# Four GNN layers over 64 graphs on one core: layer 3's transposes written to DRAM in one piece, the last graph's end in halves, new ranks for the planner, and the second graph's exponentials transposed through DRAM

## The chip, the cores and the metric

The kernel runs on one core of a Trainium2 chip. The time is the device time of one execution in microseconds (us). Before the change it is 2665.98 us, the median of three runs (2665.81 to 2669.04).

## The reference

64 graphs, each with 256 nodes, 256 features and a 256 x 256 adjacency matrix, go through four layers. Each layer computes x = layernorm(x + layer(x, adj)), all in float32.

```python
# layer 0: 4 heads, sigmoid attention scaled by degree
att = sigmoid(q @ k.T * hd ** -0.5); adj_h = adj[:, None] * att
dis = deg ** -0.5                       # deg = adj_h.sum(-1)
y = layernorm((dis[:, None] * adj_h * dis[None, :]) @ leaky(x @ W + b)) * g + b
# layer 1: 8 heads, softmax masked by adj > 0
y = softmax(where(adj > 0, q @ k.T / sqrt(hd), NEG)) @ v @ Wo + bo
# layer 2: y = silu(rmsnorm((eps * x + adj @ x) @ W1 + b1) * w) @ W2 + b2
# layer 3: one head
e = leaky(s1[:, None] + s2[None, :], 0.2)
y = gelu(layernorm(softmax(where(adj > 0, e, NEG)) @ (x @ W)) * gamma + beta)
```

## The kernel before

A graph's 256 nodes are two blocks of 128 partitions. `graph` (L340) writes down the operations of one graph with `op(engine, cost, fn, writes, reads, ...)`; nothing is emitted yet. `Plan.order` (L184) then plays all 64 graphs through a list scheduler: for each engine it keeps a clock, it takes the ready operation with the smallest key (start time plus `LEAD`, then due time plus `RANK`), and `emit` (L845) issues the operations in the order of their planned starts. So the order on every engine, SP's queue of DMAs included, is fixed by the costs in the `op` calls, by the tables `RANK` and `LEAD` (one number for each kind of operation), by `AHEAD`, `STAY`, `TURN_STAY` and by the buffers in `SLOTS`. Each engine runs its own list in that order and waits on semaphores; a late operation holds up all that stand behind it.

In the middle of the run the order is periodic: all four layers are on the way at once, each for another graph. TensorE (PE) runs float32 matmuls of 128 x 256 in two passes. Some of its operations use only a part of the array's rows or columns: L550 (scores of layer 0, 64 rows), L631 (scores of layer 1, 32 rows, two halves of 8 matmuls), L568 (degrees, 32 columns), L590 (layer 0's product, 64 columns), L667 (layer 1's product, 32 columns), L733 (mean square of layer 2, 32 columns). L365 is a transpose by PE. All others (L421, L432, L702, L714, L755, L770) use the full array. The planner adds `CHANGE` when PE goes from one of these modes to another, and `join` (L142) can tie an L733 to the L631 of another graph.

Which line makes what: L421 q and k of layers 0 and 1 (and v, output and attention products by `token_major`, L432); L702 adj @ x; L714 and L755 the two matmuls of layer 2; L770 x @ W of layer 3, with the two columns for s1 and s2; `normed` (L460) is the layer norm: L445 the statistics on VectorE (DVE), L453, the power -0.5 on GpSimd (POOL) at L455, L464, and the scaling on ScalarE (ACT) at L468; `plus` (L482) adds the residual.

A transpose is made in one of two ways. By PE: `transposed` (four 128 x 128 transposes into PSUM) and an ACT `copy`. Or through DRAM: `far_transposed` (L373) transposes 32 x 32 blocks on DVE (L377), writes them to a DRAM tile `far` and reads them back in another order. For layer 3 (`in_order=True`) these are four writes (L383) and four reads (L387); for layer 0's y one write (L391) and four reads (L393). Layer 1's exponentials take the same way for a pair of heads: DVE L652, one write L654, four reads L656. `NEAR = 1, 2, 3` says which graphs go by PE instead: the first one in layer 0, the first two in layer 1 (L640 to L648), the last three in layer 3 (L761, L784).

The end of a graph is L785 to L792: the product of layer 3, `stats`, `affine`, gelu, the sum with x, `normed` and the output's write, each over all 256 nodes at once. For the last three graphs (`ENDS`) ACT does a part of DVE's work (L468, L493).

Of the kernel before, what the change touches and what calls it, by code (L numbers as in the profile page):

```python
# [9 lines left out]
AF = mybir.ActivationFunctionType  # L10
OP = mybir.AluOpType

P = 128
# [16 lines left out]
AHEAD = 12.7  # L30
STAY, TURN_STAY = 197, 988
NEAR = 1, 2, 3
# [7 lines left out]
SLOTS = {"s": 42, "d": 10, "b": 3, "c": 72, "p": 8, "h": 8, "t": 5, "w": 3, "f": 8}  # L40
DRAM = "hf"

RANK = [
    3.44, -1.34, 0, 0.79, 3.63, 0, 7.06, 0, 0, 2.3, -1.09, 0.34, 2.1, 0.78, 0.47, 0, -8.07, 0, -2.5, 0, 15.95,
    3.93, 0.83, -0.82, -4.23, -2.95, 1.61, -7.35, 4.27, 6.06, 1.96, 5.09, -16.2, 5.57, 0.49, -0.6, 0, 0.29, 0.2,
    0, 8.07, 0, 0.26, 0, 0, -8.02, -0.52, 0.34, -5.71, 0, 1.06, -2.37, 0.99, -8.94, 0, 0, -4.56, -2.34, -6.61,
    0.36, 0.84, -1.13, 0.53, 4.6, -1.2, -1.71, 0, 0, 0, -0.62, 4.15, -3.45, -2.5, -0.12, 6.63, 0.18, 0, 0.38,
    -0.79, -2.84, 0, -12.65, 1.3, 0, -1.96, 1.34, -1.62, 20.11, -1.52, 0, -0.8, -2.32, -1.64, 0, -1.22, -15.66,
    0, -6.95, -2.98, 0, 0.05, -1.56, -0.82, -0.77, -6, -2.56, -2.91, -11.65, -5.25, -1.35, -5.62, 0.33, 0, 0.59,
    -0.44, -28.89, -6.83, 0, 0.4, 0, 0.46, 0.76, 0, 0, 12.94, -5.14, 4.78, 3.27, 0.41, -2.4, -1.34, 0, -0.87,  # L50
    -1.92, 0, -2.52, 0, -10.08, -2.01, 3.32, 0.57, -18.67, -3.41, 0, 4.56, 5.08, 3.05, -3.62, 0, 3.39, -0.48,
    -0.64, -0.1, -3.66, 19.76, -6.53, 16.91, 0, -3.84, -1.2, 0.37, -12.68, 0, -6.52, 5.03, 11.31, 6.22, 1.25,
    -5.4, 5.28, 9.76, 2.05, -0.81, -6.1, 0.74, -0.33, -6.78, -1.35, 0.27, 2.67, -2.73, 0.77, -0.98, -12.61, 0,
    1.81, 1.44, 1.4, -0.43, -5.6, 1.17, 0, -3.52, -0.14, -0.86, -0.05, -0.51, 0, 25.51, 0, 0, 0, -2.88, 0, 0, 0,
    -0.4, -0.07, 0, 0, 2.29, 0, 0, -2.22, -0.14, 1.6, 0.52, -0.32, -2.95, 0, 0, 0, -0.56, 0, -0.75, 8.73, 0, 0,
    0, 0.27, 9.58, -7, 0.78, 1.68, 0, -0.23, -10.25, -9.94, 0, 2.37, 3.11, -1.12, 0.31, -0.32, 0, -2.88, -2.04,
    0, -2.34, -0.49, -1.73, -1.73, -3.1, -1.77, 1.2, -3.97, 0.04, -0.58, -3.77, -19.26, 1.61, 0, 2.15, 0, 1.75,
    -9.45, 0, -11.3, -4.22, -40.55, -11.19, -1.7, 0, -1.02, 20.28, 2.54, 0, 0, -11.95, -3.71, 4.81, 4.78, 0, 1.6,
    0, 0, 0, -4.09, 0, -20.33, 0.55, 0.76, 0, 0, -5.26, 0.23, 2.23, 0.95, 0.44, -0.83, -0.57, -4.63, -0.68,
    -0.52, 11.56, 0.73, 0, 0, 5.95, 1.53, -1.94, 0, 1.27, 0.18, 0, -0.41, -3.03, -5.78, -1.03,  # L60
# [3 lines left out]
    0, 0, 0, 4, 0, 21, 963, 0, 0, 0, 63, 0, 36, -156, 0, 241, -51, 5, -54, -409, 0, 480, 0, -31, 0, 0, -1244, 5,  # L64
    0, 581, -13, 104, -75, 53, 0, 0, 0, 0, 0, 0, 0, 0, 0, 0, 0, 100, 0, 0, 0, 0, -88, -216, 0, -127, 0, 0, 0, 0,
    0, 0, 0, 0, 0, 0, 0, 0, 0, 0, 0, 0, 0, 73, 0, -648, -13, 0, 0, 0, 0, 0, 243, 0, 0, 0, 0, 0, 0, 52, 0, 0, 0,
    0, 0, 0, 0, 0, 0, -1022, -191, 0, 0, 0, -79, 0, 13, -157, 0, 0, 0, 0, 0, 0, 0, 0, 0, 0, 0, 0, 0, 0, 0, 0, 0,
    0, -14, -96, -46, -142, 175, -7, -49, -988, -8, 0, 0, 0, 0, -3, 56, -31, 223, 0, 72, -40, -885, 811, -10, 0,
    0, 0, 0, -181, 559, -5, 0, 0, 323, 144, 0, 239, -109, 0, 0, -40, 0, -97, -886, 230, 144, -105, 0, 2, -92, 38,
    -275, 0, 0, 0, 0, 0, -262, 0, 0, 0, -468, -319, 0, 0, 0, 0, -390, 256, 267, 0, 0, 0, 0, 0, 42, 0, 0, 0, 0, 0,  # L70
    -325, 0, 0, 0, 0, 0, -236, 0, -117, -279, 0, 0, -1, 0, 0, 0, 0, 0, 0, 0, 0, -14, 0, 0, 0, 0, 0, 0, 0, 0, 0,
    0, 0, 0, 0, 0, 0, -261, -256, 0, 0, 0, 0, 0, 0, 0, 0, -139, 0, 0, 37, 0, 0, 0, 0, 0, -156, 0, 0, 0, 0, 0, 0,
    0, 0, 0, -25, 0, 262, -10, 105, 0, 0, 0, 0, 0, -34, -107, -53, -189, -141, -364, 0, 0, -161, -46, -115, 0,
    -12, 0, -883, 0, 0, 0, 0, 0, 0, -109, -14, 0, 187, 0, -13, 721, 0, 0, -68, -68, 0, -58, 0, -31, 417, 0, 227,
]

# [40 lines left out]
class Plan:  # L117
# [66 lines left out]
    def order(self):  # L184
# [17 lines left out]
        while ready:  # L202
            best = None
            for op in ready:
# [10 lines left out]
                for kind, n in need.items():  # L215
                    free = self.free[kind]
                    if len(free) < n:
                        break
                    start = max(start, sorted(free)[n - 1][0])
                else:  # L220
                    key = start + LEAD[op.rank], op.due + RANK[op.rank], op.graph, op.index
                    if best is None or key < best[0]:
                        best = key, start, op
# [116 lines left out]
def graph(plan, nc, c, t, out, b):  # L340
# [14 lines left out]
    def load(name, src):  # L355
        v = Value("s", name, 2)
        op("SP", 470, lambda: nc.sync.dma_start(two(v), t[src][b].rearrange("(n p) d -> p n d", p=P)), [v], after=5000, size=256)
        return v
# [14 lines left out]
    def far_transposed(src, name, in_order=True):  # L373
# [509 lines left out]
```

## Time and profile before

| what | value |
|---|---|
| median of three runs | 2665.98 us |
| the profiled execution's own time | 2665.97 us |
| its span, first to last instruction | 2664.2 us |
| PE busy (matmuls) | 2629.6 us, 17248 records |
| DVE busy | 2463.8 us |
| ACT busy | 2246.5 us |
| POOL busy | 640.5 us |
| DMA packets | 764628, 502.48 MB |
| weight load of 128 x 128 (L714), mean | 190 ns |
| DVE 32 x 32 transposes of 128 x 512 (L377), mean | 671 to 713 ns |

The page's first part gives busy times; its second cuts the span into 40 slices and shows the busy share of each engine in tenths; its fourth part follows the chain that ended last. The windows view gives busy times by stretch, the timeline shows instructions in order of time with their starts, and the waits view lists who waited for whom. A matmul record has a modelled end and overlaps the next, so the work on PE is read here from the distances between starts.

### The profile page before, as it was taken

The page shows a single profiled execution, that of the slowest core. Times are in us where ns is not written, and L with a number is a line of the kernel's source. Part 1 is how long each engine was busy: PE and PEld are TensorE (multiplying, and loading weights), DVE is VectorE, ACT ScalarE, POOL GpSimd, SP SyncE. Part 2 cuts the span into 40 slices and gives each one's busy share as a digit, 9 for nine tenths or more (in the row PEclk, how much of TensorE's full clock was granted, in tenths as well). Part 3 has the DMA queues.
Part 4 walks back from the last instruction along what each step waited for, and adds up shares of the span by engine and source line. Part 5 has one row for each costly group of instructions (what it writes and reads, how often), then busy time and mean ns, then how long its engine had stood idle before and what let it go on. Part 6 is the DMA issues. An engine that isn't in the chain of part 4 may idle for free.

```text
span 2664.2 us, 54927 instructions
## 1 busy us (share of the span) xinstructions
PE 2629.6 (99%) x17248; PEld 2122.6 (80%) x17248; DVE 2463.8 (92%) x6905; ACT 2246.5 (84%) x5343; POOL 640.5 (24%) x1029
## 2 busy tenths in 40 slices
PE   8999999999999999999999999999999999999997
PEld 6777888888887888888888878878888887877786
DVE  6799999999999999999999999999999999989976
ACT  4888888888888888988888888889889888888886
POOL 1122222222222222222222222222222222222222
PEclk9999999999999999999999999999999999999998
DMA  4577777776777777777767777777677776676761
GB/s 142 153 210 199 196 206 188 200 202 182 210 195 187 197 200 192 200 189 200 200 187 206 196 186 202 196 188 200 193 195 203 188 199 183 178 198 186 212 162 38
DMA packets 764628, 502.48 MB, mean 189 GB/s; under 512 B 383792, under 2 KB 724144, under 8 KB 764336
## 3 DMA queue, kind: packets, MB, share of 16 engines
q1 hardware_dynamic: 764336, 498.97, 69.7%
q8 instruction: 137, 2.24, 0.4%
q14 instruction: 155, 1.27, 0.2%
HBM read 301.35 MB, written 197.39 MB: 187 GB/s over the span
## 4 chain that ended last, share of the span: by engine, by line
PE 89%; DVE 5%; DMA 2%; SPq 1%; issue 1%; ACT 1%; POOL 1%; POOLq 0%; DVEq 0%; ACTq 0%
PE ps L432 16%; PE ps L755 15%; PE ps L421 15%; PE ps L714 15%; PE ps L631 5%; PE ps L702 4%; PE ps L550 4%; PE ps L590 4%; PE av L667 4%; PE ps L770 4%; PE ps L365 1%; PE ps L568 1%; DVE mv L445 1%; DVE e L513 1%; DMA eT<-far 1%
## 5 line engine op out<-in xcount | busy, mean ns | idle before, releaser
L518 ACT ACTIVATE e<-e,low 128x256 f32<-128x256 f32 x1152 | 576.4, 503 | 156.9 <-DVE low L513 150.9
L455 POOL TENSOR_TENSOR mv<-mv,mhalf 128x2 f32<-128x2 f32 x384 | 313.7, 822 | 965.7 <-DVE mv L453 759.8
L714 PE MATMUL ps<-aggT,w 128*128 128x256 f32 x2048 | 463.8, 379 | 0.0
L755 PE MATMUL ps<-w,hT 128*128 128x256 f32 x2048 | 456.4, 380 | 0.0
L755 PEld LDWEIGHTS ps<-w,hT 128*128 128x128 f32 x2048 | 387.8, 190 | 56.1 <-issue 2.7
L714 PEld LDWEIGHTS ps<-aggT,w 128*128 128x128 f32 x2048 | 387.3, 190 | 56.6 <-issue 1.9
L513 DVE CUSTOM_DVE_ANT_0 e<-ps,adj 128x256 f32<-128x256 f32 x1024 | 361.9, 418 | 29.7 <-PE ps L631 28.1
L652 DVE STREAM_TRANSPOSE eb<-e 128x1024 f32<-128x1024 f32 x248 | 305.2, 1232 | 2.5 <-ACT e L518 0.4
L721 ACT ACTIVATE hT<-ps,br,r 128x256 f32<-128x256 f32 x512 | 259.5, 576 | 1.8 <-PE ps L755 0.9
L719 ACT ACTIVATE sq<-ps,b 128x256 f32<-128x256 f32 x512 | 218.2, 469 | 24.1 <-PE ps L714 23.9
L468 ACT ACTIVATE x<-y,mv 128x256 f32<-128x256 f32 x384 | 215.4, 595 | 18.2 <-DVE mv L464 18.1
L518 ACT ACTIVATION_READ_ACCUMULATOR e<-e,low 128x1 f32 x1152 | 220.8, 192 | 0.0
L445 DVE BATCH_NORM_STATS2 mv<-y 128x6 f32<-128x512 f32 x320 | 217.3, 692 | 0.6
L556 DVE TENSOR_TENSOR att<-att,adjT 128x512 f32<-128x512 f32 x256 | 164.7, 682 | 9.1 <-ACT att L554 8.9
L741 POOL TENSOR_TENSOR rs<-rs,mhalf 128x2 f32<-128x2 f32 x64 | 45.4, 709 | 521.2 <-DVE rs L739 519.8
L576 POOL TENSOR_TENSOR dp<-dp,mhalf 128x8 f32<-128x8 f32 x64 | 126.6, 1978 | 161.6 <-DVE dp L575 161.3
L745 DVE TENSOR_TENSOR hT<-hT,pr 128x1024 f32<-128x1024 f32 x128 | 149.1, 1202 | 2.2 <-POOL pr L405 2.1
L631 PE MATMUL ps<-kT,qT 32*128 32x256 f32 x2048 | 147.8, 400 | 0.0
L554 ACT ACTIVATE att<-ps 128x512 f32<-128x512 f32 x256 | 138.8, 600 | 3.9 <-PE ps L550 3.2
L726 DVE TENSOR_TENSOR sq<-sq 128x512 f32<-128x512 f32 x192 | 130.9, 682 | 9.1 <-ACT sq L719 8.8
L421 PE MATMUL ps<-x0T,w_k 128*128 128x256 f32 x512 | 131.9, 385 | 6.1 <-DMA w_k<-in_L_gnn_W_k 6.1
L747 ACT ACTIVATE hT<-hT 128x1024 f32<-128x1024 f32 x128 | 133.3, 1051 | 3.4 <-DVE hT L745 2.7
(116 smaller groups left out, 5460.9 us busy)
## 6 DMA issues: line engine op xcount, KB each, us to landing
far<-eb SPq DMA_DIRECT2D x248, 512.0 KB, 3.1
eT<-far SPq DMA_DIRECT2D x992, 128.0 KB, 4.1
adj<-in_adj SPq DMA_DIRECT2D x128, 256.0 KB, 5.8
far<-eb SPq DMA_DIRECT2D x488, 64.0 KB, 2.4
x<-in_x SPq DMA_DIRECT2D x64, 256.0 KB, 5.1
x0T<-in_xT SPq DMA_DIRECT2D x64, 256.0 KB, 5.0
adjT<-in_adjT SPq DMA_DIRECT2D x64, 256.0 KB, 5.5
adj<-in_adjT SPq DMA_DIRECT2D x64, 256.0 KB, 5.6
```

The costliest lines, as they stand in the source:

```text
L421: pe.matmul(two(ps)[:, o, :], w.t[:, k, o * P:(o + 1) * P], two(xT)[:, k, :], start=(k == 0), stop=(k == DB - 1))
L432: pe.matmul(two(ps)[:, n, :], two(xT)[:, k, n * P:(n + 1) * P], w()[:, k, :], start=(k == 0), stop=(k == DB - 1))
L445: op("DVE", 615, lambda: dve.bn_stats(mv.t[:, :6], src.t[:, :512].rearrange("p (n c) -> p c n", n=NB)), [mv], [src])
L455: op("POOL", 720, lambda: pool.tensor_tensor(m()[:, :, 0], m()[:, :, 0], c.mhalf[:, :NB], OP.pow), [mv], [mv], after=400)
L513: op("DVE", 345, lambda n=n: dve.tensor_tensor_reduce(out=E(n), in0=two(logits)[:, n, :], in1=two(negmask)[:, n, :], scale=-scale, scalar= ...
L518: op("ACT", 491, lambda n=n: act.activation(E(n), E(n), AF.Exp, bias=low.t[:, n:n + 1], scale=-1.0, accum_out=r.t[:, col(n):col(n) + 1]), ...
L631: pe.matmul(two(pss[i])[:, n, :], two(qT1)[s, hq, n * P:(n + 1) * P], two(kT1)[s, hq, :], start=True, stop=True)
L652: op("DVE", 1155, lambda e=e, eb=eb: dve.transpose(eb.t.rearrange("p (b g i) -> p g b i", b=4, i=32), e.t.rearrange("p (g b i) -> p g b i" ...
L714: pe.matmul(two(ps)[:, i, :], c.w2_1.t[:, k, (j + i) * P:(j + i + 1) * P], two(aggT)[:, k, :], start=(k == 0), stop=(k == DB - 1))
L719: op("ACT", 357, lambda ps=ps, sq=sq, i=i, j=j: act.activation(two(sq)[:, i, :], two(ps)[:, i, :], AF.Square, bias=c.b2_1.t[:, j + i:j + i ...
L721: op("ACT", 491, lambda ps=ps, i=i, j=j: act.activation(Hb(j + i)[:, 0], two(ps)[:, i, :], AF.Identity, bias=c.br2.t[:, j + i:j + i + 1], ...
L755: pe.matmul(two(ps)[:, n, :], Hb(j)[:, 0, n * P:(n + 1) * P], c.w2_2.t[:, j, :], start=(j == 0), stop=(j == HB - 1))
```

## The change

Line numbers of the changed kernel differ; the diff below shows the code. It does five things.

1. Layer 3's transposes through DRAM. `far_shuffled` takes the place of `far_transposed(in_order=True)`: one DVE transpose, whose output is written in steps of two elements (node pairs interleaved), one write to DRAM in pieces of 64 floats in place of four writes in pieces of 128 floats, and four reads in pieces of 64 floats in place of 32. The transposed tile holds its 256 columns in another order, so the matmuls of layer 3 take their stationary operand with a step of two elements (`ordered_block`). For the last three graphs, which go by PE, `near` makes the same order with two ACT copies of a half each.
2. The last graph's end (`last`): product, statistics (`bn_stats` and `bn_aggr`), power, two DVE operations, gelu, sum, statistics, power, scaling by DVE and output's write for each half of 128 nodes by itself.
3. `NEAR = 1, 1, 3`: the second graph's exponentials of layer 1 go through DRAM.
4. New `RANK`, `LEAD`, `AHEAD`, `STAY` and `TURN_STAY`, a new table `LIKING` that is added to the key of PE's operations by the mode before and their own, and new buffer counts.
5. New costs in many `op` calls. They change the planned order only.

```diff
-AHEAD = 12.7
-STAY, TURN_STAY = 197, 988
-NEAR = 1, 2, 3
+AHEAD = 12.2
+STAY, TURN_STAY = 286, 657
+NEAR = 1, 1, 3
...
-SLOTS = {"s": 42, "d": 10, "b": 3, "c": 72, "p": 8, "h": 8, "t": 5, "w": 3, "f": 8}
+SLOTS = {"s": 44, "d": 10, "b": 3, "c": 36, "p": 8, "h": 8, "t": 5, "w": 3, "f": 8}
...
+LIKING = {("rows", "full"): -28, ("rows", "columns"): -93, ("rows", "transpose"): 200, ("columns", "full"): 68, ("columns", "rows"): -118, ("columns", "columns"): -28, ("columns", "transpose"): -46, ("transpose", "full"): -277, ("transpose", "rows"): -90, ("transpose", "columns"): -10, ("transpose", "transpose"): -58}
...
-                    key = start + LEAD[op.rank], op.due + RANK[op.rank], op.graph, op.index
+                    lead = LEAD[op.rank] + (LIKING.get((mode, op.mode), 0) if op.engine == 'PE' else 0)
+                    key = start + lead, op.due + RANK[op.rank], op.graph, op.index
...
+    def far_shuffled(src, name):
+        eb, far, dst = Value("s", "eb"), Value("h", "far"), Value("s", name, 4)
+        op("DVE", 635, lambda: dve.transpose(
+            eb.t.rearrange("p (b k i n) -> p k n b i", b=4, k=2, n=NB),
+            src.t.rearrange("p (n k b i) -> p k n b i", n=NB, k=2, b=4)), [eb], [src])
+        F = lambda: far.t[:64].rearrange("(b k r) (p m) -> b k (r p) m", b=4, k=2, m=64)
+        op("SP", 470, lambda: nc.sync.dma_start(
+            F().rearrange("b k p m -> p (b k) m"), eb.t.rearrange("p (g m) -> p g m", m=64)), [far], [eb], after=2900, size=220)
+        for q in range(4):
+            op("SP", 590, lambda q=q: nc.sync.dma_start(
+                dst.t[32 * q:32 * q + 32].rearrange("j (g m) -> j g m", m=64),
+                F()[q].rearrange("k (a j) m -> j (k a) m", a=4)), [(dst, q)], [far], after=2800, size=64)
+        return dst
+    def near(src, name):
+        ps, dst = transposed(src), Value("s", name, 2)
+        for k in range(DB):
+            op("ACT", 357, lambda k=k: act.copy(
+                two(dst)[:, k, :].rearrange("p (i n) -> p n i", n=NB),
+                two(ps)[:, k, :].rearrange("p (n i) -> p n i", n=NB)), [(dst, k)], [ps])
+        return dst
+    def ordered(ap):
+        return ap.rearrange("p (i n) -> p n i", n=NB)
+    def ordered_block(ap, n):
+        return ordered(ap)[:, n]
...
+    def last(n, eT, v3, V3, r, x):
+        ps, st, y, o = Value("p", "ps"), Value("c", "mv"), Value("w", "y"), Value("w", "o")
...
+        op("DVE", 328, lambda: dve.bn_stats(st.t[:, :6], ps.t[:, :D]), [st], [ps])
+        def fn():
+            dve.bn_aggr(st.t[:, 6:8], st.t[:, :6])
+            for _ in range(2):
+                dve.tensor_tensor(root(), root(), r1(), OP.mult)
+            dve.tensor_scalar(root(), root(), 1e-5, None, op0=OP.add)
+        op("DVE", 600, fn, [st], [st, r])
+        power()
...
+        op("SP", 470, lambda: nc.sync.dma_start(out[b].rearrange("(n p) d -> p n d", p=P)[:, n, :], o.t), [], [o], after=2300, size=128)
...
-    xT3 = copy(transposed(x), "xT3") if b >= plan.graphs - NEAR[2] else far_transposed(x, "xT3")
+    xT3 = near(x, "xT3") if b >= plan.graphs - NEAR[2] else far_shuffled(x, "xT3")
...
-                pe.matmul(ps.t[:, :D + 2], two(xT3)[:, k, n * P:(n + 1) * P], c.w3.t[:, k, :],
+                pe.matmul(ps.t[:, :D + 2], ordered_block(two(xT3)[:, k, :], n), c.w3.t[:, k, :],
...
-    eT = copy(transposed(e), "eT") if b >= plan.graphs - NEAR[2] else far_transposed(e, "eT3")
-    ps = token_major(eT, lambda: V3()[:, :, :D], [v3])
+    eT = near(e, "eT") if b >= plan.graphs - NEAR[2] else far_shuffled(e, "eT3")
+    if b == plan.graphs - 1:
+        for n in range(NB):
+            last(n, eT, v3, V3, r3, x)
+        return
+    ps = token_major(eT, lambda: V3()[:, :, :D], [v3], ordered_block)
```

## The prediction

> **What bounds the kernel now.** I read the page first (parts 1, 2 and 4):
>
> ```profile
> span 2664.2 us, 54927 instructions
> ...
> PE 2629.6 (99%) x17248; PEld 2122.6 (80%) x17248; DVE 2463.8 (92%) x6905; ACT 2246.5 (84%) x5343; POOL 640.5 (24%) x1029
> ...
> PE   8999999999999999999999999999999999999997
> ...
> PE 89%; DVE 5%; DMA 2%; SPq 1%; issue 1%; ACT 1%; POOL 1%; POOLq 0%; DVEq 0%; ACTq 0%
> ```
>
> PE is full in all slices but the first and the last, and makes 89% of the chain. DVE's 92% overstates it: in the timeline DVE operations of 0.68 us start every 0.60 us. Second, the windows view: is PE ever idle?
>
> ```profile
> 0.00:100.00 100.00, 91.22 (x614) 71.46 (x615) 62.03 (x180) 62.92 (x147) 13.65 (x16) 0.98 0.38 117
> ...
> 300.00:400.00 100.00, 100.00 (x668) 81.42 (x667) 95.93 (x263) 88.40 (x204) 25.17 (x41) 1.00 0.77 208
> ...
> 2300.00:2400.00 100.00, 97.58 (x616) 76.83 (x615) 87.41 (x244) 82.59 (x196) 22.43 (x34) 1.00 0.74 198
> ...
> 2600.00:2664.00 64.00, 45.97 (x228) 37.83 (x226) 41.94 (x118) 41.26 (x87) 18.12 (x39) 0.88 0.15 38
> ```
>
> From 300 to 2300 us PE has no gap; a graph takes 40.64 us (L755's runs in the chain start at 1280.65 and 1321.29). There only work taken from PE shortens the time. At both ends it is waits. Third, the PE timeline of one period:
>
> ```profile
> 1287.39 1.03 PE L432 MATMUL ps<-w_v,xT 128*128 128x256 f32 x4
> 1288.35 2.00 PE L550 MATMUL ps<-qT,kT 64*128 64x256 f32 x16
> 1290.28 1.93 PE L667 MATMUL av<-eT,v 128*32 128x256 f32 x32
> 1292.03 0.62 PE L568 MATMUL ps<-added,ones 128*32 128x128 f32 x16
> 1292.58 1.13 PE L432 MATMUL ps<-w_l,x0T 128*128 128x256 f32 x4
> 1293.55 1.89 PE L432 MATMUL ps<-w_o,yT 128*128 128x256 f32 x8
> ...
> 1300.89 1.89 PE L421 MATMUL ps<-xT,w_q 128*128 128x256 f32 x8
> 1302.71 1.95 PE L590 MATMUL ps<-att,v 128*64 128x256 f32 x16
> 1304.59 0.32 PE L733 MATMUL ps<-sq,mean_of 128*32 128x64 f32 x8
> 1304.84 1.15 PE L631 MATMUL ps<-kT,qT 32*128 32x256 f32 x16
> 1305.91 1.99 PE L702 MATMUL ps<-adj,x 128*128 128x256 f32 x8
> 1307.75 1.03 PE L421 MATMUL ps<-x0T,w_q 128*128 128x256 f32 x4
> ```
>
> Full-array passes start 215.85 ns apart. A block of partial modes then has a price: the distance from the full run before it to the second run behind it, less 215.85 ns for each full pass between. The first block: 1293.55 - 1287.39 - 8 x 0.21585 = **4.43 us**; the second, 1307.75 - 1300.89 - 16 x 0.21585 = **3.40**. By the same rule elsewhere: L631 alone 1.27, L365 0.44, L550 2.13 (at 20 us), L667 2.06 (at 222), L733 0.45 (at 2456), L590 2.08 (at 2348), L590 with L568 2.65 (at 31), L631 with L568 1.85 (at 134). The period is 144 x 0.21585 + 4.43 + 3.40 + 1.27 + 0.44 = 40.62: the rule holds.
>
> Applied to all of PE's order, the prices sum to 2618.3 us. So the span is 6.1 (first weights) + 2618.3 + 24.3 (idle between matmuls) + 15.5 (behind the last) = 2664.2. Comparing each run's start with the sum up to it, the idle is 10.9 before 300 us, 1.3 in the middle, 7.2 from 2300 to the last L755 at 2632, 4.9 after.
>
> **The change, part by part.**
>
> *PE's steady order.* In the changed program's order a period has the blocks {L550, L667}, {L365}, {L733, L631}, {L631, L590, L568}. Neighbours save about 0.20 each against single prices (L631 then L568: 1.27 + 0.77 - 1.85), so: 2.13 + 2.06 - 0.20 = 3.99; 0.44; 0.45 + 1.27 - 0.20 = 1.52; 1.27 + 2.65 - 0.20 = 3.72. Together 9.68 against 9.54: **+0.14 us a graph**, 46 periods, +6.3.
>
> *The second graph through DRAM.* 32 transposes fewer on PE, 0.11 each: -3.5; eight ACT copies (L646, 0.589) fewer off the path. It adds four L652 (1.23 on DVE), four writes (3.1 to landing) and sixteen reads (4.1) on SP. The wait added is L667's on the reads. From that graph's second L631 to its L667 lie 35.3 us of PE work (28.9 before). The chain: 16 exponentials at 0.50 = 8, 1.2, 3.5, 4 x 0.43 + 4.1 = 5.8, some 18.5 us. Cost 0; if early DVE and ACT queues were as full as for the third graph (40 us seen) 4.
>
> *PE's ramps.* The same pricing of the whole new order gives 2619.9: +6.3 - 3.5 - 1.1 for fewer lone blocks. **PE work +1.6.**
>
> *Strided stationary operands.* L770 and layer 3's L432 load weights with step 2: 1024 passes. No row shows this. Nearest below: L714's contiguous load, 190 ns, hidden in the 216 ns pass; above: twice that, 380, or 164 ns bare a pass, 168 us. I take 0, since the moving operand of L667, read in runs of 32, shows no slower pace; a gain is excluded, the load being hidden already.
>
> *Strided DVE transposes.* L377's 0.66 to 0.71 contiguous is one end, double the other: +1.4 us a graph on DVE. Taken: 0, covered by DVE's waits; without cover see the first rival.
>
> *Single writes.* L383 occupies SP for 0.455 us four times, then 2.4 to landing; one L391 takes 0.53 and 2.5. Eight issues a graph become two: the way through DRAM is some 1.7 us shorter. Hidden: from L755 to L770 lie 26.1 us of PE work (25.9 before), from L770 to the product 37.3 (35.4). Behind the one write on SP stand loads and other transposes' DMAs, which also move up. Value 0 in the middle. In packets: 2048 of 128 B at 13 ns and 512 of 512 B at 27 become 2048 of 256 B at 18, so the 16 engines' load hardly changes. [...] Were a 256 B write as dear as one of 512, it would be 0.6 us a transpose by an estimate from these rows, still hidden.
>
> *Idle at the start, 10.9.* L421's 1.8 at 9.7 us (weights): SP's new order loads w_q, x0T, w_k first, no x between; 0.8 left. Two waits in
>
> ```profile
> PE ps L365 <- ACT x L468: 3.2, 3, 2.6
> PE ps L590 <- DVE mv L453: 1.5, 1, 1.5
> ```
>
> The first's 2.65 (at 64.8) goes: that graph's L590 had 16.7 us of PE work before its transpose, now 24.8, above the 20.8 it got with the wait. Late next are the transposes of the first graph's exponentials: 1.45 stays. Of L590's 1.5 I keep 1.0; L667's 1.0 (at 148) goes; of 3.2 smaller ones 2.0 stay. New: the first L550 has 0.9 us behind its q (1.9 seen): +1; the sixth graph's L568 6.0 behind L550 (7.9 seen): +1. Sum 7.2, bounds 4 and 13.
>
> *Idle later.* Middle 1.3. Late: distances are like before's, but 17.1 once from L770 to the product (19.9 seen) and 7.3 from the last L733 to L755 (9.0): 6 of 7.2, bounds 4 and 9. After the last L755: two half copies in `near` (L774's 0.376 twice against L412's 0.585): 5.0.
>
> *The end.* From the first half of the last product to the scaled output took 12.3 us. By halves I lay DVE's new list at rows' rates (0.38 for half a L445, 0.17 for each small one and for the unseen `bn_aggr`, which may take 0.06 to 0.42; POOL's power on one column 0.50, from 0.71 for two and 1.98 for eight): 12.0. DVE still carries the two other graphs' ends in between, so halving gains little. The write of 128 KB in place of 256 (3.1): 2.7. Behind the last matmul 14.8, bounds 13.5 and 16.5.
>
> **Sum:** 6.1 + 2619.9 + 7.2 + 1.3 + 6.0 + 5.0 + 14.8 = 2660.3 us of span. The profiled execution's own time was 2665.97, 1.8 above its span and equal to the median, so **2662.0 us**, 0.15% less. About 0.2%, 5.3 us, is what a measurement of this kernel can tell from no change.
>
> **Rivals.**
>
> *PE stalls once a graph (slower).* Three distances shrink in the steady order: from the output product (L432, w_o) to L702 10.7 to 7.3 us, from L590 to its transpose 32.9 to 25.9, from L702 to L714 3.9 to 1.5. The first is tightest. Its chain on DVE, with what stands between: plus 0.60, added 0.60, transpose 0.64, L445 0.64, three small to middle ones 0.8, transpose 0.64, L453; power 1.0 with its semaphores; L464; two L468 1.1; some 6.8. Half a microsecond is spare. Both transposes in it are strided: doubled, they add 1.3 and PE stalls 0.8 a graph. For it: DVE starts nothing out of order. Against: before, DVE waits for PE at L513 (28.1 us), so it isn't behind. It is slower than before from 0.09 us a graph, 0.2% slower from 0.2; at 0.5 it gives 2662 + 46 x 0.5 = 2685. Chance 0.15.
>
> *The ends gain more.* Idle at the lower bounds and the end at 13.5: 2662 - 3.2 - 2 - 1.3 - 1 = 2654.5. For it: most stalls of before are single late operations. Chance 0.17.
>
> *The new ranks do nothing for the ends.* Idle stays 24.3: 2666.8. Chance 0.15.
>
> *Strided weights leave their cover.* 2662 + 168 = 2830 at twice the load time; it bites from 216 ns on. [...] Chance 0.05.
>
> **How the numbers follow.** The forecast has 0.48; its own range is 2656 to 2668, and 0.19 of it lies below 2660.7. Faster: 0.17 + 0.19 = 0.36. Same: 0.29 + 0.15 = 0.44. Slower: 0.15 + 0.05. The range goes from 2652 to 2679 (a stall of 0.37 a graph); it leaves out strided weights, larger stalls and a little below.
>
> **What would show it.** PE's period from L755 to L755: 40.77 if the block prices hold, more if PE stalls, and then an idle of PE before L702, L365 or L714 once a graph. Weight loads of L770 at 190 ns. PE's first L365 of the third graph without a wait. Packets near 705,000 with 128 B ones gone. Wrong would make it a period that differs from 40.77, or an idle at the ends outside 15 to 27.

## The result, and the profile after

The changed kernel takes **2675.82 us** (median of six runs, 2674.66 to 2677.73); the kernel before takes 2665.99 beside it. The ratio is 1.0041 [1.0031, 1.0051]: 0.41% slower, where 2662.0, 0.15% less, was forecast. The profiled execution took 2674.66 us, its span is 2672.9.

First the page of the changed kernel: span, busy time, PE's slices, the chain, packets.

```profile
span 2672.9 us, 54596 instructions
...
PE 2633.3 (99%) x17216; PEld 2123.2 (79%) x17216; DVE 2439.1 (91%) x6923; ACT 2257.2 (84%) x5338; POOL 597.3 (22%) x1031
...
DMA packets 699201, 506.62 MB, mean 190 GB/s; under 512 B 378272, under 2 KB 658208, under 8 KB 698912
...
PE 87%; DVE 7%; DMA 2%; ACT 2%; issue 1%; POOL 1%; SPq 0%; ACTq 0%; DVEq 0%; POOLq 0%
```

Nothing new bounds the kernel. PE's share of the chain fell from 89% to 87%, DVE's rose from 5% to 7%: PE waits more. Where, the PE timeline of a period and the windows tell (start, us, engine, line).

```profile
1288.01 7.07 PE L819 MATMUL ps<-w,hT 128*128 128x256 f32 x32
1295.01 2.00 PE L614 MATMUL ps<-qT,kT 64*128 64x256 f32 x16
1296.93 1.93 PE L731 MATMUL av<-eT,v 128*32 128x256 f32 x32
1298.80 1.99 PE L456 MATMUL ps<-w_l,x0T 128*128 128x256 f32 x8
1300.63 1.89 PE L456 MATMUL ps<-w_o,yT 128*128 128x256 f32 x8
...
1328.79 1.46 PE L819 MATMUL ps<-w,hT 128*128 128x256 f32 x6
```

The period is 1328.79 - 1288.01 = 40.78 us (forecast 40.77). The block of L614 and L731 (L550 and L667 before) costs 1300.63 - 1288.01 - 40 x 0.21585 = 3.99 (forecast 3.99). So PE has no stall in the steady state and the prices of the modes are right. The windows (busy us and instructions of PE, PEld, DVE, ACT, POOL; PE's clock, DMA share, GB/s):

```profile
0.00:100.00 100.00, 93.64 (x631) 73.17 (x632) 68.73 (x198) 64.11 (x147) 13.26 (x16) 1.00 0.47 144
100.00:200.00 100.00, 92.28 (x622) 71.66 (x621) 87.59 (x244) 78.07 (x196) 20.14 (x27) 0.97 0.81 224
300.00:400.00 100.00, 98.50 (x639) 79.95 (x641) 95.08 (x263) 85.60 (x195) 26.67 (x41) 1.00 0.79 222
2300.00:2400.00 100.00, 99.33 (x616) 81.35 (x616) 96.85 (x268) 88.72 (x209) 24.41 (x37) 1.00 0.65 191
```

The same stretch of the kernel before:

```profile
100.00:200.00 100.00, 97.44 (x681) 74.59 (x680) 93.28 (x266) 84.97 (x211) 19.46 (x27) 1.00 0.77 220
```

The loss lies between 100 and 200 us, where PE is busy 92 us of 100, against 97 before, and where its mean clock is 0.97, against 1.00. The same sum as in the forecast gives for both kernels what follows. "PE work" is the sum of the prices of all passes and blocks; "idle" is how much later a matmul starts than the priced work ahead of it allows; the columns of idle are the stretches up to 310 us, from there to 2235 us, and from there to the last matmul.

| us | first weights | PE work | idle to 310 us | to 2235 us | behind that | behind the last matmul | span |
|---|---|---|---|---|---|---|---|
| before | 6.1 | 2618.3 | 11.1 | 0.8 | 12.4 | 15.4 | 2664.2 |
| forecast | 6.1 | 2619.9 | 7.2 | 1.3 | 11.0 | 14.8 | 2660.3 |
| after | 5.6 | 2619.9 | **17.7** | 1.5 | 11.9 | 16.3 | 2672.9 |

Of the 12.6 us between forecast and measurement 10.5 are idle at the start. PE's waits in the changed kernel (total, times, longest):

```profile
PE ps L445 <- DMA w_k<-in_L_gnn_W_k: 5.5, 1, 5.5
PE ps L370 <- ACT x L492: 4.2, 1, 4.2
PE av L731 <- DMA eT<-far: 2.8, 1, 2.8
```

The first is the first weights. The second stands at 122 us: the fourth graph's transpose, on its x of layer 0. The third stands at 181 us: layer 1's product, on exponentials read back from DRAM. And the transfers: the windows of the DMA alone (clock, DMA share, GB/s), first of the kernel before, then of the changed one.

```profile
90.00:100.00 10.00, 1.00 0.10 32
100.00:110.00 10.00, 1.00 0.70 149
110.00:120.00 10.00, 1.00 0.86 286
```

```profile
90.00:100.00 10.00, 1.00 0.94 303
100.00:110.00 10.00, 1.00 0.88 242
110.00:120.00 10.00, 1.00 0.98 274
```

The second graph's exponentials add 4 x 512 KB of writes and 16 x 128 KB of reads, and they fall into the stretch in which the kernel before left the DMA engines nearly idle and then filled them by itself. That gave the first theory, **A**: the way through DRAM makes the start late, by SP's queue. Its rival, **B**: the new order alone does it, whatever way the exponentials take.

### The profile page after: what moved, and what is told of

It reads as the page before. It is cut to its first block, busy times and chain, and to the rows that moved or that the text cites. A ratio compares the mean times of both kernels' runs of the same rounds, so it can differ in the third digit from the quotient of the medians.

```text
span 2672.9 us, 54596 instructions
## 1 busy us (share of the span) xinstructions
PE 2633.3 (99%) x17216; PEld 2123.2 (79%) x17216; DVE 2439.1 (91%) x6923; ACT 2257.2 (84%) x5338; POOL 597.3 (22%) x1031
## 2 busy tenths in 40 slices
DMA packets 699201, 506.62 MB, mean 190 GB/s; under 512 B 378272, under 2 KB 658208, under 8 KB 698912
## 3 DMA queue, kind: packets, MB, share of 16 engines
q14 instruction: 153, 1.25, 0.2%
## 4 chain that ended last, share of the span: by engine, by line
PE 87%; DVE 7%; DMA 2%; ACT 2%; issue 1%; POOL 1%; SPq 0%; ACTq 0%; DVEq 0%; POOLq 0%
PE ps L778 16%; PE ps L819 15%; PE ps L456 15%; PE ps L445 15%; PE ps L695 4%; PE ps L654 4%; PE ps L614 4%; PE av L731 4%; PE ps L766 4%; PE ps L834 4%; DVE e L537 2%; PE ps L632 1%; PE ps L370 1%; DVE mv L469 1%; DMA eT<-far 1%
## 5 line engine op out<-in xcount | busy, mean ns | idle before, releaser
L479 POOL TENSOR_TENSOR mv<-mv,mhalf 128x2 f32<-128x2 f32 x382 | 301.6, 794 | 1196.9 <-DVE mv L477 837.6
L778 PE MATMUL ps<-aggT,w 128*128 128x256 f32 x2048 | 470.1, 382 | 1.7 <-ACT att L618 0.9
L785 ACT ACTIVATE hT<-ps,br,r 128x256 f32<-128x256 f32 x512 | 268.2, 568 | 27.5 <-PE ps L654 27.5
L618 ACT ACTIVATE att<-ps 128x512 f32<-128x512 f32 x256 | 132.9, 604 | 2.6 <-PE ps L614 1.9
L445 PE MATMUL ps<-x0T,w_q 128*128 128x256 f32 x512 | 132.6, 382 | 0.0
```

The costliest lines, as they stand in the source:

```text
L445: pe.matmul(two(ps)[:, o, :], w.t[:, k, o * P:(o + 1) * P], two(xT)[:, k, :], start=(k == 0), stop=(k == DB - 1))
L479: op("POOL", 690, lambda: pool.tensor_tensor(m()[:, :, 0], m()[:, :, 0], c.mhalf[:, :NB], OP.pow), [mv], [mv], after=200)
L778: pe.matmul(two(ps)[:, i, :], c.w2_1.t[:, k, (j + i) * P:(j + i + 1) * P], two(aggT)[:, k, :], start=(k == 0), stop=(k == DB - 1))
L785: op("ACT", 491, lambda ps=ps, i=i, j=j: act.activation(Hb(j + i)[:, 0], two(ps)[:, i, :], AF.Identity, bias=c.br2.t[:, j + i:j + i + 1], ...
```

## The experiments

In every experiment the planner's keys are the planned starts of the kernel that it is made from, so that what is not edited keeps its order on each engine. "Order of before" and "order of after" mean that. Line numbers in a diff of keys are those of that kernel's own code, and the first number is the graph, from 0. Each ratio is to the kernel before on the same chip. The columns of idle come from one profile each. Two pairs of kernels with equal lists up to the last graph (before and `b_halves`, after and `a_whole`) differ by 2.9 and 3.5 us in the idle up to 310 us, so a difference of 3 us there is not evidence by itself; the ratios are.

| label | us | ratio | PE work | idle to 310 | behind 2235 | behind last matmul |
|---|---|---|---|---|---|---|
| a_pe | 2677.11 | 1.0046 [1.0033, 1.0058] | 2623.4 | 14.7 | 12.0 | 16.2 |
| b_dram | 2675.60 | 1.0037 [1.0024, 1.0049] | 2614.6 | 23.9 | 13.7 | 14.9 |
| b_single | 2661.23 | 0.9986 [0.9977, 0.9995] | 2618.3 | 10.8 | 6.6 | 17.3 |
| a_modes | 2673.34 | 1.0029 [1.0018, 1.0040] | 2614.2 | 19.3 | 13.4 | 16.3 |
| b_halves | 2668.44 | 1.0007 [0.9999, 1.0016] | 2618.3 | 14.0 | 10.6 | 18.8 |
| b_sh | 2664.80 | 0.9999 [0.9991, 1.0008] | 2618.3 | 14.9 | 6.0 | 18.4 |
| b_all | 2672.94 | 1.0027 [1.0016, 1.0039] | 2614.6 | 24.9 | 7.0 | 18.4 |
| a_whole | 2679.38 | 1.0052 [1.0039, 1.0064] | 2619.9 | 21.2 | 11.8 | 16.8 |
| b_queue | 2672.60 | 1.0029 [1.0018, 1.0041] | 2614.6 | 20.1 | 13.7 | 14.9 |
| a_chain | 2675.99 | 1.0042 [1.0029, 1.0054] | 2623.4 | 14.3 | 12.2 | 16.3 |
| a_fix | 2678.68 | 1.0051 [1.0038, 1.0063] | 2619.9 | 21.4 | 12.1 | 16.3 |
| b_soon | 2659.83 | 0.9984 [0.9975, 0.9993] | 2618.3 | 12.0 | 6.1 | 17.3 |
| b_early | 2667.31 | 1.0012 [1.0004, 1.0021] | 2614.6 | 17.8 | 8.9 | 14.8 |
| a_early | 2671.61 | 1.0032 [1.0020, 1.0043] | 2619.9 | 12.8 | 11.9 | 16.3 |
| b_traffic | 2672.01 | 1.0029 [1.0019, 1.0040] | 2618.3 | 16.5 | 13.9 | 14.9 |
| b_best | 2663.41 | 0.9993 [0.9984, 1.0001] | 2618.3 | 13.3 | 6.4 | 17.3 |
| b_part | 2666.93 | 1.0006 [0.9997, 1.0014] | 2614.6 | 19.4 | 6.5 | 17.2 |
| a_early_modes | 2664.58 | 0.9998 [0.9990, 1.0007] | 2614.2 | 12.4 | 11.9 | 16.3 |

### One part at a time

`a_pe`: the order of after, the second graph's exponentials by PE.

```diff
-NEAR = 1, 1, 3
+NEAR = 1, 2, 3
```

> The changed kernel with its order kept, but the second graph's exponentials of layer 1 transposed by TensorE again (32 transposes of 0.11 us more on it, 16 reads and 4 writes fewer on SP). Theory A (the way through DRAM overfills SP's queue between 85 and 130 us, so the fourth graph's reads come late and TensorE waits 4.2 us at 122): that wait and the 3.0 at 181 go, 3.5 us of work come back, the time falls to 2670 to 2673. Theory B (the new order of the ends costs the time whatever way the exponentials take): the waits stay and the time rises by the 3.5 us of work to 2679.

`b_dram`: the order of before, with only this edit the other way round.

```diff
-NEAR = 1, 2, 3
+NEAR = 1, 1, 3
```

> The kernel before with its order kept, and only the second graph's exponentials of layer 1 sent through DRAM. Theory A: SP's queue falls behind from 90 us on, TensorE waits, 2670 to 2675 although 3.5 us of transposes are gone. Theory B: the transposes go and nothing else moves, 2662 to 2664.

`b_single`: the order of before, with only `far_shuffled`, `near` and `ordered_block` for layer 3.

```diff
+        if in_order and SINGLE:
...
+            op("SP", 470, lambda: nc.sync.dma_start(
+                F1().rearrange("b k p m -> p (b k) m"), eb.t.rearrange("p (g m) -> p g m", m=64)), whole, [eb], after=2900, size=220)
...
-                pe.matmul(ps.t[:, :D + 2], two(xT3)[:, k, n * P:(n + 1) * P], c.w3.t[:, k, :],
+                pe.matmul(ps.t[:, :D + 2], ordered_block(two(xT3)[:, k, :], n), c.w3.t[:, k, :],
```

> The kernel before with its order kept, and only layer 3's way through DRAM changed: one write, strided transposes and strided stationary operands, two half copies for the last three graphs. Both theories: the period stays at 40.64 us, weight loads at 190 ns; SP issues six DMAs fewer a graph, hidden: 2665 to 2667. If the single write is what costs, 2669 or more.

`b_dram` shows the way through DRAM to be dear in the order of before: +0.37% although PE has 3.7 us less to do. That speaks for A. `a_pe` speaks for B: without that way the new order is as slow as with it. Single writes are not hidden: they alone make the kernel before 0.14% faster, by 5.8 us less idle behind 2235 us against 1.9 us more behind the last matmul.

`b_halves`, `b_sh`, `b_all`: the order of before with the halved end; with it and single writes; with both and the way through DRAM. `a_whole`: the order of after with the end whole again.

```diff
-    if b == plan.graphs - 1:
+    if HALVES and b == plan.graphs - 1:
```

> The kernel before, in its order, with only the last graph's last product, softmax and output in two halves (strided stationary operand and single writes left out). Theory C (the halved end is worth what was priced): behind the last matmul 14.8 in place of 15.4 us, idle otherwise as before, 2663.5 us against 2664.3. Rival D (the two half copies and 32 small operations delay the end): idle after the last L755 grows from 4.9 to 6 or more, 2665.5 us.

> The kernel before, in its order, with layer 3's single writes and the halved end together; the second graph's exponentials stay on PE and the ranks are not new. Theory E (the parts add): 2661.2 of the single writes alone, less 0.8 for the halves: 2660.5 us. Rival D (halves delay the end): 2662.5.

> The whole change in the order of before: single writes, halved end, second graph's exponentials through DRAM, but no new ranks. Theory E (parts add: single writes -3.1 us, DRAM way +9.3 to +11.3, halves about -0.8): 2670 us, and the new ranks are then what costs the other 6 us of after. Theory F (the DRAM way costs less where single writes empty the SP queue; it is late there only because the queue is full from 103 to 120 us): 2663 to 2666 us. Rival G (the DRAM way is what makes after slow whatever the order): 2674 to 2676.

> The changed kernel in its order, with only the last end whole again as in the kernel before. Theory C (halves worth 0.6 to 1 us): 2676.6 us. Rival D (halves delay the end, which shows 16.3 behind the last matmul against 15.4): 2674.5 us.

In the order of before the halved end gives nothing: behind the last matmul 18.8 us in place of 15.4, with 1.8 less idle ahead of it, and with single writes 18.4 in place of 17.3. Only the second pair prices the halves: in `b_halves` the last product itself ran at a granted clock of 0.50 (its eight matmuls took 3.78 us, in `b_single` and `b_sh` 2.00). In the order of after the whole end is 0.5 us longer; the rest of `a_whole`'s ratio lies in the start, where the lists are the same. By the ratios the halves cost 0.13% (`b_sh` against `b_single`) or gain 0.11% (the changed kernel against `a_whole`), with intervals that overlap, so their sign is not shown. `b_all` comes out between theories E and F: the whole change without its ranks is 0.27% slower, and with them 0.41, with intervals that overlap.

### Who waits for the transfers

In `b_dram` one wait of PE makes most of it. Three of PE's waits, and the longest of DVE from 100 to 131 us, in that run:

```profile
PE ps L652 <- DVE mv L475: 7.9, 1, 7.9
...
PE ps L693 <- DVE low L535: 1.9, 1, 1.9
...
PE ps L454 <- DVE dp L637: 1.8, 1, 1.8
```

```profile
DVE y L663 <- DMA rb<-far: 5.7, 1, 5.7
```

L652 (L590 before) stands at 129 us behind the fourth graph's x of layer 0 on DVE, and that behind y, L663 (L601 before), which needs yT from DRAM. SP's queue of `b_dram` shows when the yT reads were issued; in the kernel before they went at 99.18, 101.96 and 102.95:

```profile
105.78 0.38 SPq L404 DMA_DIRECT2D yT<-far  x1
110.95 0.47 SPq L404 DMA_DIRECT2D yT<-far  x1
113.83 1.13 SPq L404 DMA_DIRECT2D yT<-far  x2
```

So the wait is not that of the graph that takes the way. The way's reads stand on SP's queue ahead of another graph's reads. `b_queue` puts only those others forward:

```diff
+    for n in range(4):                                  # yT reads of the fourth graph
+        out[3, ((404, "SP"), n)] = 93400.0 + n
+    out[1, ((739, "SP"), 0)] = 93500.0                  # write of rT of the second
```

> The run with the order of before and the second graph's exponentials through DRAM (2675.6 us, PE waiting 8.05 us at 129 us), with one more edit: on SP's queue the fourth graph's four reads of yT and the second graph's write of rT are put behind the second group of four eT reads, so that the yT reads are issued from about 101 us instead of 105.8 to 115. Theory H (SP issues one transfer every 0.47 us, the queue is full from 103 to 120 us, and the yT reads stand late in it): the y on DVE starts at 112.0, where DVE ends its other work, not at 117.8; the wait falls from 8.05 to about 2.3 and the time to about 2670. Rival I (it is the DMA engines' load or DVE's own list): the wait stays above 6, 2675.

SP's timeline of `b_queue`, and then DVE's (in brackets the idle time before, and what ended it):

```profile
101.55 1.74 SPq L404 DMA_DIRECT2D yT<-far  x4
```

```profile
111.75 0.43 DVE L663 TENSOR_TENSOR y<-yT,dis 128x256 f32<-128x256 f32 x1
...
118.27 0.43 DVE L335 SCALAR_TENSOR_TENSOR scratch<-w,a 128x256 f32<-128x256 f32 x1 [3.41 <-DMA a<-in_L_gnn_a]
```

y starts at 111.75, as expected (112.0), though the rb reads that the profile of `b_dram` had named as the releaser are issued up to 114: the named one was only the last of several. But behind y stands L335, which needs a load that is itself late on SP (issued at 114.39). PE's wait fell from 7.9 to 4.9 us and the time by 3.0, half of what was expected. `b_early` takes that out too (with `AHEAD` at 60 when the new order is made, so that the loads may go early):

```diff
+    for key in ((329, 0), (289, 5), (289, 6), (289, 7), (289, 8), (283, 8)):
+        out[0, ((key[0], "SP"), key[1])] = 62000.0      # six loads of weights
```

> The run with the order of before, the second graph's exponentials through DRAM and the fourth graph's yT reads pulled forward (2672.6 us, PE waiting 5.09 at 125 us; y started at 111.75 as forecast, but then DVE stood 3.41 us at L335 for the load of a, which SP issued at 114.39). One more edit: six loads of weights that SP issued between 102 and 135 us go out at 60 to 63 us. Theory H (the wait at 125 to 129 us is SP's full queue, whichever transfer is late on it): the wait falls to 1.7 to 2.5, the time to 2669 to 2670. Rival I (DVE's list or the DMA engines): 2672 to 2673.

The wait of L652 is 2.1 us, the ratio 1.0012 in place of 1.0037. The wait at L652 follows what stands on SP's queue: `b_queue` changed little but the places on it. (Moving the loads out takes their traffic from the DMA engines there too, though the DMA share was no lower, 0.77 and 0.92 from 100 to 120 us against 0.66 and 0.89 in `b_dram`; which of the two counts more there the runs don't separate.) The gain is more than expected although PE now waits 4.1 us at 92 us, behind a DVE that stood 2.4 us for an adjacency matrix. The counter-test, `b_traffic`, leaves all engines' work in the kernel before as it is and adds the traffic alone, into tiles that nobody reads:

```diff
+                if TRAFFIC and b == 1:
+                    far, spare = Value("h", "far"), Value("d", "spare", 4)
+                    op("SP", 470, ... dma_start(far.t, e.t), [far], [e], ...)
+                    for q in range(4):
+                        op("SP", 470, ... dma_start(spare..., far...), [(spare, q)], [far], ...)
```

> The kernel before, unchanged in PE's, DVE's and ACT's work, with only the traffic of the second graph's DRAM way added: its four writes of 512 KB (of the exponentials as they lie) and its sixteen reads of 128 KB into tiles that nobody reads. Theory H (the traffic on SP's queue is what costs, not the latency of the way, nor DVE's four added transposes): a wait of 4 to 8 us appears at 120 to 130 us, time 2670 to 2673. Rival M (the cost is the way's own latency and DVE's transposes): 2665 to 2666.5.

The DMA's window, DVE's waits and PE's waits of `b_traffic`:

```profile
90.00:100.00 10.00, 1.00 0.96 277
```

```profile
DVE y L663 <- DMA yT<-far: 3.1, 1, 3.1
```

```profile
PE ps L652 <- DVE mv L475: 4.6, 1, 4.6
```

The traffic alone costs 0.29%, with the longest wait at the same place. So rival M, the way's own latency and DVE's four added transposes, is not the whole cost. It is not out either. By its ratio `b_dram` lost 9.9 us net of the 3.7 that PE saved, some 13.6 in all; `b_traffic` lost 7.7. And `b_dram` has two waits that `b_traffic` has not: 1.8 us at 90 us and 1.9 at 107 (L454 and L693), both for DVE, on which added transposes of 1.24 us start at 87.15 and 101.29 us.

### The order of after

`a_pe` was no quicker without the way. Its lists tell why. Its yT reads were issued at 98.98, but DVE did not take up y (L666) before 118.41. DVE's timeline of `a_pe`:

```profile
115.17 0.45 DVE L637 STREAM_TRANSPOSE deg<-ps 128x256 f32<-128x256 f32 x1 [1.67 <-PE ps L633]
117.65 0.17 DVE L642 SCALAR_TENSOR_TENSOR dis<-deg,dp 128x8 f32<-128x8 f32 x1 [0.36 <-POOL dp L641]
118.41 0.42 DVE L666 TENSOR_TENSOR y<-yT,dis 128x256 f32<-128x256 f32 x1
```

y stands behind the fifth graph's degree chain, since the planner, with the way's reads on SP, had set it late, and my `a_pe` kept that place. So it could not tell A from B. `a_chain` is `a_pe` with y's chain 7 us earlier:

```diff
+    return {(g, k): s - 7000 if g == 3 and 111000 < s < 122000 and k[0][0] in (666, 466, 470, 474, 476, 480, 489, 493, 526, 529) else s ...}
```

> The run with after's order and the second graph's exponentials by PE (2677.1 us), with the fourth graph's first layer's end (y, statistics, normalization and the two writes of x: ten small operations of DVE, POOL and ACT) ordered 7 us earlier, ahead of the fifth graph's degree chain on DVE; its yT reads have landed by 104 us there, and y starts only at 118.4. Theory J (the 4.24 us wait of the transpose at 122 to 128 us is the order of DVE's list, which was planned around late yT reads): the wait goes, the time falls by 3 to 4 us to 2673.5. Rival K (what is put behind, the degree chain and the wide softmax, is late next by as much): within 1.5 us of 2677.

The 4.24 us wait went, y started at 111.11, and the time stayed (1.0042): six waits of 0.6 to 1.5 us between 119 and 154 us stand there now, where `a_pe` had one of 0.7 beside the long one. Rival K holds. `a_fix` makes the same repair in the changed kernel, with the yT reads put forward on SP:

> The changed kernel with the same repair: the fourth graph's yT reads go on SP's queue before 5 of the second graph's eT reads and four loads (issued from about 98 us instead of 103.4 to 108.5), and its first layer's end stands 5 us earlier in the lists. Theories H and J together: y starts at about 107 us instead of 112.65, the 4.24 us wait at 122 us goes, the time falls by 3 to 5 us to 2671 to 2673. If the delay only moves to the eT reads that are now later, the wait at 181 us stays or grows and the time is 2675 to 2677.

It gained nothing either (1.0051): the delay moved to the eT reads, 3.3 us of wait at 184 us. `a_early` also takes the six loads out of that stretch, as in `b_early`:

> The changed kernel with the repair that did not pay (yT reads forward on SP, the fourth graph's y chain 5 us earlier in the lists, 2678.7 us with 3.5 us of wait for eT reads at 184 us and 2.4, 1.4, 1.8 at 116 to 124), and the same six loads of weights at 60 to 63 us instead of 95 to 117. The DMA engines' share in after was 0.94, 0.88, 0.98, 0.71, 1.03 in the five 10 us stretches from 90 to 140 us (before: 0.10, 0.70, 0.86, 0.97, 0.93). Theory L (what stalls PE there is that SP's queue and the DMA engines are full): idle up to 310 us falls by 4 to 6 us, time 2672 to 2674. Rival K (DVE and ACT can't do this order's work any faster there): 2677 to 2679.

Now the start's idle is 12.8 us, the 3.3 us wait for eT is gone, and the ratio is 1.0032, against 1.0051 of `a_fix`, with intervals that overlap a little. Theory L holds in the profile, and in the time with a margin of little more than the noise; against the changed kernel itself (1.0041) the gain is not clear of it. What was left is PE's own order. `a_modes` had moved the degree product L632 and its four small operations in graphs 8 to 52 about 20 us later, behind L731, where PE is in column mode already:

```diff
+    for g in range(8, 53):
+        to = min(s for s in by[727, "PE"].values() if s > by[610, "PE"][g + 1])
+        later = to + 2000 - by[630, "PE"][g]
+        for kind in ((630, "PE"), (637, "DVE"), (640, "DVE"), (641, "POOL"), (642, "DVE")):
+            out[g, (kind, 0)] = by[kind][g] + later
```

> The changed kernel with its order kept but for graphs 8 to 52, whose degree matmul (L632 of the changed kernel) and the four small operations behind it are moved some 20 us later, from behind the layer 0 product to behind the layer 1 product. By the block prices the period falls from 40.78 to 40.64 us: 44 x 0.14 = 6.2 us less, 2669.6. If instead waits set the period, it stays at 40.78 and the time at 2675.8.

Its work fell by 5.7 us as priced, but some 3 us of it came back as idle. The same move from graph 10 on, on top of `a_early`:

> The changed kernel with the queue repaired (2671.6 us, ratio 1.0032) and the degree products of graphs 10 to 52 moved behind the next graph's L731, so that PE has four blocks of modes a period with one seam more: work 2614.2 in place of 2619.9 us by the block prices. If the block prices hold and the start is now free of the queue: 2666, ratio 1.0011, a period of 40.65. If, as with the same move in the unrepaired order, idle grows by what the work loses: 2669 to 2671.

Two periods in its PE timeline:

```profile
1319.87 7.07 PE L820 MATMUL ps<-w,hT 128*128 128x256 f32 x32
1360.51 7.07 PE L820 MATMUL ps<-w,hT 128*128 128x256 f32 x32
```

The period is 40.64 us, the span 2662.0 (6.2 less than `a_early`, 5.7 priced), the ratio 0.9998. With the start's repair and the blocks' the changed kernel is as fast as the one before: together they give back its 0.41%. How the 0.41 divides between them the ratios tell only roughly, 0.09 by the first and 0.34 by the second; the spans 4.7 and 6.2 us.

### What beats both

`b_soon` adds to `b_single` a place 2 us earlier for the second graph's first x:

```diff
+    return {(g, k): s - 2000 if g == 1 and 52000 < s < 64000 and k[0] in ((467, "DVE"), (471, "DVE"), (477, "POOL"), (486, "DVE"), (490, "ACT"), (526, "DVE")) else s ...}
```

> The kernel before with layer 3's single writes (2661.2 us), and the second graph's first x (six small operations of DVE, POOL and ACT) ordered 2 us earlier, ahead of part of the first graph's softmax. If PE's 2.65 us wait at 64.9 us and the 4.1 us behind it are this chain's order: about 2659. If the first graph's exponentials and their transposes are late next: 2661 to 2662. In both it tells whether single writes alone are faster than before on a second chip: ratio 0.9985.

At 0.9984 [0.9975, 0.9993] it is faster than both kernels; nearly all of it is the single writes, as the idle around the 2.65 us wait fell by 1.5 and other waits grew. `b_best` adds the early loads, `b_part` puts single writes onto `b_early`:

> The kernel before with layer 3's single writes and the second graph's first x ordered 2 us earlier (2659.8 us, ratio 0.9984), and six loads of weights issued from 68 us instead of between 100 and 135. If SP's full queue between 100 and 150 us also costs that kernel its waits of 0.9 at 118 and 3.2 at 149 us (L590, behind reads from DRAM): 2657 to 2658. If not: 2660.

> Single writes and the second graph's exponentials through DRAM in the order of before, with both repairs of SP's queue (yT reads forward, six loads of weights early): without the single writes this took 2667.3 us, ratio 1.0012. Theory E (single writes are worth 3.1 us there too, by a shorter end): 2664, ratio 0.9999; the way through DRAM, which takes 3.7 us of work from PE, then still gives nothing. If the single writes free the queue as well: 2661 or below.

Both missed. In `b_best` DVE waits for an adjacency matrix, whose load SP now issues at 84.48 us, behind the weights, in place of 75.50 in `b_soon` (DVE's waits from 80 to 100 us):

```profile
DVE adj L546 <- DMA adj<-in_adj: 4.5, 1, 4.5
```

and PE loses 5 us from 90 to 97 us. The kernel before has no full queue there to repair, so moving loads only moves the lateness. `b_part` shows the way through DRAM to give nothing even when it is repaired.

## Why the prediction was wrong

The step that failed is the idle of PE at the start: 7.2 us forecast, 13 at most, 17.7 measured, 10.5 of the 12.6 us that are missing. Two terms of it were wrong, the cost of the second graph's way through DRAM, put at 0, and the new order's waits, taken from the old list. The other terms came out within 1.5 us each. The prediction's own sign of being wrong came, an idle at the ends outside 15 to 27: it is 17.7 + 11.9 = 29.6.

- **PE's steady order** was right: period 40.78 (40.77), blocks 3.99 (3.99). The +0.14 us a graph is real, and moving the degree product gives it back.
- **Strided stationary operands** were right, and **strided DVE transposes**. The groups of the changed kernel:

```profile
L819 PEld LDWEIGHTS ps<-w,hT 128*128 128x128 f32 x2048 | 387.6, 190 | 58.1 <-issue 2.6 <-ACT hT L811 2.5 <-ACT x L492 0.4
L834 PEld LDWEIGHTS ps<-w,xT 128*128 128x128 f32 x512 | 99.7, 196 | 13.2 <-ACT xT L412 1.2 <-DVE sq L790 0.7 <-issue 0.3
```

```profile
L396 DVE STREAM_TRANSPOSE eb<-e 128x512 f32<-128x512 f32 x61 | 43.2, 708 | 0.8 <-ACT e L542 0.7
```

  With a step of two L834 (L770 before) loads in 196 ns against 190 contiguous, within the 216 ns pass. The strided transposes take 708 ns, inside the 671 to 713 of before. Packets: 699,201 against 705,000.
- **The second graph through DRAM, cost 0, at most 4**: this step failed. It compared the way's length (18.5 us) with the PE work ahead of the product that needs it (35.3), and that wait indeed did not come. It left out what stands behind the sixteen reads on SP's queue, and that the stretch from 100 us on is where the DMA engines are filled already (share 0.70 to 0.97 from 100 to 140 us in the kernel before). In the order of before `b_dram` prices it at 0.37% net of the PE work saved, and `b_traffic` the traffic alone at 0.29%. In the new order the price is not shown: `a_pe`, without the way, was no faster. What shows there, in one profile each, is that the idle at the start goes from 17.7 to 12.8 us when the queue is relieved and the fourth graph's chain set earlier (`a_early`); that is still not less than before the change (11.1).
- **Idle at the start, 7.2 (bounds 4 and 13)**: measured 17.7. The step struck waits from the list of before one by one and let the rest stand, as if a new order kept them. (The waits that it lists for before add up to 11.6, not to the 10.9 that it divides.) The 2.65 us wait at 64.8 did go, as forecast, and the two waits of about 1 us for the first L550 and the sixth graph's L568 did not come. But the new lists had their own: 4.2 at 122, 2.8 at 181. Behind both PE's clock was half for 3.4 us, which the forecast put at nothing: the mean of 0.97 from 100 to 200 us is some 3 us by an estimate. `a_chain` and `a_fix` show that such a wait is not worth its length: remove it and the next late operation takes its place.
- **Single writes, 0 in the middle**: right there. What failed is that they were given nothing at the end, where there is no next graph to hide a transpose: -0.14% in the order of before (-0.08 in `b_sh` against `b_halves` and -0.06 in `b_part` against `b_early`, inside the intervals). In the order of after that gain doesn't show (11.9 us of idle behind 2235, against 12.4 before).
- **The end**: 16.3 against 14.8, inside its bounds (13.5 to 16.5). Late idle: 11.9 against 11.0.
- **The rivals**: the ranks do nothing for the ends (2666.8, chance 0.15) was nearest in kind, but none had a start that gets worse. Both slower rivals, a stall in each graph and strided weight loads that leave their cover, were placed in the steady state, where nothing went wrong. The measured time lies in the stated range (2652 to 2679) by the room left for such a stall, which is luck.

What stays open: how much of the changed kernel's idle is due to the way through DRAM, what the new buffer counts do (no run tries them alone), the sign of the halved end, and why equal lists differ by 3 us of idle at the start. Of the 3.5 us between `a_whole` and the changed kernel most can be read: its wait at 185 us was 4.2 in place of 2.8 us, and behind each of the two long waits half the clock lasted longer (to 128.1 and 189.5 us, against 126.5 and 184.5), some 1.4 us more in all. Why the transfer came later there is not shown.

## What to carry to other kernels

A way through DRAM is paid also by whoever stands behind it on the queue that issues it: in `b_dram` another graph's yT reads were issued at 105.78 to 113.83 us in place of 99.18 to 102.95, and PE waited 7.9 us. Before you call it hidden, list the transfers that move up behind it and who waits for these, and look at the DMA share of that very stretch, not at the mean.

In a start where several engines' lists are full, a single wait's length is no price: in `a_chain` a wait of 4.24 us went and the ratio fell only from 1.0046 to 1.0042. Estimate by what the stretch as a whole can carry, and bound a new order's idle from above by more than the waits that you can see in the old one.

## What the runs showed of the hardware

A wait of PE can cost more than itself. In PE's timeline of `b_queue` the sixteen matmuls of L652 took 3.68 us after 4.92 us of idle, and 1.95 in the steady state before (L590).

```profile
125.39 3.68 PE L652 MATMUL ps<-att,v 128*64 128x256 f32 x16 [4.92 <-DVE mv L475]
```

The changed kernel's L731 behind its two long waits, at 122 and 181 us, against 1.93 in the steady state:

```profile
122.69 3.29 PE L731 MATMUL av<-eT,v 128*32 128x256 f32 x32
...
181.25 3.59 PE L731 MATMUL av<-eT,v 128*32 128x256 f32 x32 [2.81 <-DMA eT<-far]
```

The windows behind such waits show why (busy us and instructions of PE, granted clock): `b_queue` behind 4.92 us of idle, the changed kernel behind 2.81 (181 us), the kernel before behind 2.65 (65 us).

```profile
125.00:129.00 4.00, 3.61 (x17) 0.50 0.71 230
```

```profile
181.00:185.00 4.00, 3.75 (x33) 0.57 0.22 51
```

```profile
65.00:68.00 3.00, 3.00 (x14) 0.53 0.93 289
```

The clock is half there: in the changed kernel 0.50 from 123.11 to 126.52 and from 181.13 to 184.54 us, in the kernel before from 64.4 to 67.8, each time 1.00 before and behind; in `b_queue` 0.50 from 125 to 129 us and 0.92 from 129 to 133. The matmuls of L652 and L731 above take 1.4 to 1.7 us longer. The idle beside it was 4.17 and 2.81 us in the changed kernel, 2.65 in the kernel before and 4.92 in `b_queue`. The length of one wait does not settle it: in `b_dram` 2.86 us, at 2470 us, left the clock at 1.00, and in `b_soon` waits of 1.25 and 0.69 us, at 146 and 147 us, were followed by 0.50. The forecast priced waits without this, and read the 1.45 us behind the wait at 65 us as late transposes, where the clock was 0.53.
